# A graph layer with gathered node rows: paired gather buffers, node products in the first layer's tile, another order of the step, and lags taken in over the last 17 groups

## The chip, the cores and the metric

The kernel runs on one core of one Trainium2 chip. The metric is the device time of one execution in microseconds (us); the median over the runs counts. A second source is one execution taken by the hardware profiler, whose own time is given beside its span.

TensorE is called PE, VectorE DVE, ScalarE ACT, GpSimd POOL and SyncE SP, as in the profile. PEld is PE's loading of weights, which overlaps its products.

## The reference, cut to what matters

There are 12,500 nodes with 64 features (`x`) and 200,000 edges, sorted by their target node `dst`. Each edge has 64 features and a distance.

```python
nodes    = node_state[edges].reshape(num_edges, -1)      # x[src] beside x[dst]
gates    = ssp(edge_state @ We1 + be1) @ We2 + be2
gates    = gates * (1.0 - sigmoid(5.0 * (edges_distance - 3.5)))
h        = ssp(nodes @ Wn1 + bn1) @ Wn2 + bn2
sums     = zeros.at[edges[:, 1]].add(h * gates)
new      = node_state + (ssp(sums @ Ws1 + bs1) @ Ws2 + bs2)
out      = layernorm(x + new)
```

`ssp` is softplus minus log 2. All is in fp32.

## The kernel before

**Tiling.** The edges form 391 groups of 512, each with two halves of 256 and four slots of 128. As the edges are sorted by `dst`, the targets of a half lie in a window of 42 nodes that starts at a base held in `base_i`. The half of the first node layer that belongs to `dst` is computed once per node into a table in DRAM (`x @ Wn1[64:]`, L471), and 42 rows of it per half are loaded as weights (`wns`, L204). The row of `x` for `src` is gathered by GpSimd with an indirect DMA per slot (`gather`, L166 to L178), four per group. In one group of 32 the fourth slot is fetched row by row on SP instead (`fetch`, L180). A one-hot of each edge's place in its window stands in columns 64 to 105 of the same buffer (`onehot`, L209), so that one product with `wns` adds both halves of the node layer.

**One group's path.** `load` (SP: edge features and `wns`), `gather` (POOL), `onehot` (DVE), `transposes` (PE, L217, into a tx tile of PSUM), `xcopy` (ACT, L222), `layer1_edge` and `layer1_node` (PE, L226, L228, L233, into a z tile of two PSUM banks), `exps` and `logs` (ACT, L243, L246), `softplus` (DVE, L251), `layer2_edge` and `layer2_node` (PE, L257, L260, L265, into a gh tile), `hcut` and `message` (DVE, L270, L274), `scatter` (PE, L278: message times one-hot), `window` (DVE, L287: added to `sums` at the half's base). z, gh and tx have two buffers each; `xg`, which holds the gathered rows and the one-hot, has 25.

**Order.** The order of every engine is written out by hand (`manual_schedule`). One loop step i has groups at different stages: the scatter of group i-3, the second layer of i-1, the first layer of i+1, the transposes of i+3, and the gather of i+19. On PE the order in a step is L278, L257, L260, L226, L228, L233, L217, L265. The scatter writes into an unused part of the second bank of the z tile of i+1. From step `both` = 378 on, 12 groups before the last, the lags are cut at once: step 378 has no transposes and two second layers, step 379 three scatters, each into a tx tile of its own.

**Nodes.** When all edges of a block of nodes are done (`block_steps` gives the step, with a margin that the kernel checks), its `node_block` runs in five parts, one per loop step: `hidden` (PE, L306) with `clamp` (DVE, L314, L315, and SP's load of x, L312); `logs` (ACT, L318, L319) with `ssp` (DVE, L322); `layer2` (PE, L327, L330) with `center` (DVE, L334, L336, L337); the square (ACT, L341) and its sum (DVE, L345, L346); `root` (ACT, L350, L351) and `store` (DVE, L356 to L359, SP L360). Their products go into tx tiles. There is one block of 212 nodes, 23 of 512, and two of 256 at the end, whose parts take turns after the last step.

**Start.** Up to some 72 us the table is built, the windows' bases are found and the first 20 groups' gathers begin; the later 14 of these wait for a DVE memset in the table's loop (L171). A branch at the end of the program handles edges outside of their window; it is not taken with these data.

Of the kernel before, what the change touches and what calls it, by code (L numbers as in the profile page):

```python
# [31 lines left out]

# [19 lines left out]

P = 128
# [11 lines left out]
CATCH_UP = 12  # L65
# [7 lines left out]
def node_blocks(N):  # L73

    rest = N - NB
    first = rest % NB
    assert rest > 0 and first % 2 == 0 and first <= HE
    sizes = ([first] if first else []) + [NB] * (rest // NB) + [HE, HE]
    return [(sum(sizes[:i]), n) for i, n in enumerate(sizes)]
# [18 lines left out]
def gnn_resnorm_kernel(ctx: ExitStack, tc: tile.TileContext, a: dict, out: bass.AP, E: int):  # L98
# [52 lines left out]
    half = const.tile([P, 1], F32, name="half")  # L151
    ones3 = const.tile([PIECES, HE], BF16, name="ones3")
# [13 lines left out]
    def gather(g, after=False):  # L166

        xg = loads.tile([P, K, P], F32, name="xg", bufs=AHEAD + 5)
        xgs[g] = xg
# [61 lines left out]
    def layer1_node(g, h):  # L231
        zn = zs[g][:, h, HE * (1 - h) : HE * (2 - h)]
        nc.tensor.matmul(zn, wns[:, g % REST, h, :], xTs[g][:, h], start=True, stop=True, skip_group_check=True)  # L233
# [29 lines left out]
    def layer2_node(g, h):  # L263
        for t in range(2):
            nc.tensor.matmul(ghs[g][:, 1, 2 * t + h, :], ss[g][:, 1 + h, t, :], wn2, start=False,  # L265
                             stop=h == 1 and t == 1, skip_group_check=True)
# [5 lines left out]
    def message(g):  # L272
        msgs[g] = work.tile([P, K, D], F32, name="msg", bufs=3)
        nc.vector.tensor_mul(msgs[g], ghs[g][:, 0], hs[g])  # L274
# [6 lines left out]

    def window(g):
        for h in range(2):
            base = nc.values_load(base_i[0:1, 2 * g + h : 2 * g + h + 1], engines=[DVE], min_val=0, max_val=N - 1,
                                  skip_runtime_bounds_check_because="it was clamped to these bounds")
            part = sums[h * D : (h + 1) * D, bass.ds(base, W)]
            nc.vector.tensor_add(part, part, scs[g][h * D : (h + 1) * D, h * W : (h + 1) * W])  # L287

    def node_block(first, n, pool):
# [7 lines left out]
        def tile3(name):  # L297
            return pool.tile([P, 2, 2, D], F32, name=name, bufs=2)[:p, :nq]
# [11 lines left out]
        def clamp():  # L310
            t["y"] = tile3("y")
            nc.sync.dma_start(t["y"], x[rows, :].rearrange("(q p k) d -> p q k d", q=nq, k=2))  # L312
            t["l"], t["zb"] = (pool.tile([P, HE], F32, name=name, bufs=2) for name in ("l_s", "zb"))
# [19 lines left out]
        def center():  # L333
            nc.vector.scalar_tensor_tensor(t["y"], t["y"], 2.0, t["u"][:, :nq], OP.mult, OP.add)  # L334
            mean = small("mean")
            nc.vector.tensor_reduce(mean, t["y"], AX.X, OP.add)  # L336
            nc.vector.scalar_tensor_tensor(t["y"], mean.to_broadcast([p, nq, 2, D]), -1.0 / D, t["y"], OP.mult, OP.add)  # L337
# [5 lines left out]
        def variance():  # L343
            t["v"] = small("var")
            nc.vector.tensor_reduce(t["v"], t["y2"], AX.X, OP.add)  # L345
            nc.vector.tensor_scalar(t["v"], t["v"], 1.0 / D, EPS, OP.mult, OP.add)  # L346

        def root():
            t["r"] = small("rstd")
            nc.scalar.activation(t["r"], t["v"], AF.Ln)  # L350
            nc.scalar.activation(t["r"], t["r"], AF.Exp, scale=-0.5)  # L351

        def store():

            v, r = t["v"], t["r"]
# [3 lines left out]
            nc.vector.tensor_mul(t["y"], t["y"], r.to_broadcast([p, nq, 2, D]))  # L359
            nc.sync.dma_start(out[rows, :].rearrange("(q p k) d -> p q k d", q=nq, k=2), t["y"])  # L360

        def then(f, g):
            def both():
                f()
                g()
            return both

        return [(hidden, clamp), (None, then(logs, ssp)), (layer2, center), (None, then(square, variance)),
                (None, then(root, store))]

    def node_part(part):
        if part[0]:
            part[0](tx_tile())
        part[1]()

    with tc.manual_schedule():
# [4 lines left out]
        with tc.tile_pool(name="prep", bufs=1) as prep:  # L381
# [23 lines left out]
            nc.vector.memset(half, 0.5)  # L405
            nc.vector.memset(ones3, 1.0)
# [334 lines left out]
```

## Time and profile before

| what | value |
|---|---|
| runs, median of 3 | 2591.24 us |
| lowest and highest of the runs | 2576.13 and 2596.45 us |
| the profiled execution's own time | 1999.2 us |
| its span, first to last instruction | 1997.4 us |
| mean granted clock of PE in it | 0.986 |
| ACT busy | 919.0 us, 46% of the span |
| L251, softplus on DVE | 373.2 us, 392 instructions of 952 ns |
| L243, Exp on ACT | 317.4 us, 392 of 810 ns; idle before it 975.8 us, ended by PE |
| L217, transposes on PE | 283.5 us, 1552 of 283 ns; idle before it 69.9 us, most of it ended by gathers |

The profile's page gives, for each engine, its busy time, its share of the span and its instructions; then the span in 40 slices, with each slice's busy share in tenths; then groups of instructions, one per line of the kernel and shape, with busy time, mean duration and the idle time just before them with what ended it. In a group's name "out<-in" stands for the tiles written and read. Durations of PE's products overlap: the distance between starts is what a product costs, not its row's duration. A timeline shows start, duration, engine, line and tiles in order of time, and in brackets how long the engine had been idle and what released it. A table by windows gives each engine's busy time in a stretch, and the clock that PE was granted there.

### The profile page before, as it was taken

To read this page: it belongs to the slowest core of one execution; us is meant where nothing else is said; L and a number is where in the kernel's file an instruction comes from. 1 tells how busy PE (TensorE), PEld (TensorE's weight loads), DVE (VectorE), ACT (ScalarE), POOL (GpSimd) and SP (SyncE) were. 2 spreads that over 40 slices of the span, in tenths; PEclk is the share of its full clock that TensorE was granted. 3 is DMA by queue.
4 is the path that set the end of the run, shared out by engine and by line. 5 is a ranking of instruction groups with operands and counts; after the bars stand their busy time and mean duration, and the time that the engine had idled before them with its cause. 6 is when DMAs were issued, how large, how long until landed. Compare 5 with 4: busy or idle time off the path is not lost.

```text
span 1997.4 us, 42101 instructions
## 1 busy us (share of the span) xinstructions
PE 1881.8 (94%) x11378; PEld 1505.4 (75%) x11378; DVE 1050.5 (53%) x2752; ACT 919.0 (46%) x1322; POOL 1474.1 (74%) x1555
## 2 busy tenths in 40 slices
PE   4999999999999999999999999999999999999996
PEld 4888888887777777777777777777777877777775
DVE  4455555555544545545555555555554555555555
ACT  1344545454444444444444444444454554444433
POOL 7777777777777777777777777777777777777770
PEclk9999999999999999999999999999998999999988
DMA  8432222222223223232222322232222232223220
GB/s 231 140 68 68 66 69 68 67 67 69 66 68 69 58 66 69 62 70 61 63 68 64 69 65 64 68 69 69 68 65 68 64 71 68 68 71 68 68 61 25
DMA packets 171021, 143.15 MB, mean 72 GB/s; under 512 B 46507, under 2 KB 142947, under 8 KB 170778
## 3 DMA queue, kind: packets, MB, share of 16 engines
q1 hardware_dynamic: 119778, 87.95, 15.2%
q0 software_dynamic: 49632, 50.92, 14.2%
q8 instruction: 95, 1.56, 0.3%
q10 hardware_dynamic: 1368, 1.51, 0.3%
q14 instruction: 148, 1.21, 0.2%
HBM read 130.57 MB, written 9.63 MB: 70 GB/s over the span
## 4 chain that ended last, share of the span: by engine, by line
PE 58%; DMA 20%; POOL 7%; issue 6%; ACT 4%; DVE 3%; DVEq 1%; POOLq 0%; SPq 0%; ACTq 0%
DMA xg<-in_x,src_i 19%; PE gh L265 11%; PE z L233 9%; PE gh L260 8%; PE z L228 8%; POOL xg L176 7%; PE tx L217 6%; PE z L278 6%; PE gh L257 4%; PE z L226 3%; ACT u L246 2%; ACT u L243 2%; PE z L471 2%; DVE s L251 1%; DVE sums L287 1%
## 5 line engine op out<-in xcount | busy, mean ns | idle before, releaser
L176 POOL DMA_INDIRECT xg<-in_x,src_i x1551 | 1473.9, 950 | 476.8 <-issue 310.0
L251 DVE SCALAR_TENSOR_TENSOR s<-u,z 128x768 f32<-128x768 f32 x392 | 373.2, 952 | 842.6 <-ACT u L246 776.7
L243 ACT ACTIVATE u<-z 128x768 f32<-128x768 f32 x392 | 317.4, 810 | 975.8 <-PE z L233 975.8
L233 PE MATMUL z<-xT,wns 106*128 106x256 f32 x1564 | 410.0, 384 | 0.0
L265 PE MATMUL gh<-consts,s 128*128 128x64 f32 x3128 | 394.1, 269 | 0.0
L265 PEld LDWEIGHTS gh<-consts,s 128*128 128x128 f32 x3128 | 391.6, 196 | 0.1
L246 ACT ACTIVATE u<-u,one 128x768 f32<-128x768 f32 x392 | 366.1, 934 | 12.3
L217 PE MATMUL tx<-consts,xg 128*106 128x128 f32 x1552 | 283.5, 283 | 69.9 <-DMA xg<-in_x,src_i 63.9
L233 PEld LDWEIGHTS z<-xT,wns 106*128 106x128 f32 x1564 | 301.3, 193 | 44.4 <-issue 0.4
L217 PEld LDWEIGHTS tx<-consts,xg 128*106 128x106 f32 x1552 | 194.9, 133 | 164.9 <-DMA xg<-in_x,src_i 116.1
L260 PE MATMUL gh<-consts,s 128*128 128x128 f32 x1564 | 279.9, 301 | 0.0
L228 PE MATMUL z<-eT,consts 128*128 128x256 f32 x782 | 277.9, 437 | 0.0
L260 PEld LDWEIGHTS gh<-consts,s 128*128 128x128 f32 x1564 | 205.1, 191 | 89.0 <-issue 88.3
L278 PE MATMUL z<-xg,msg 128*128 128x84 f32 x1500 | 235.4, 279 | 0.0
L222 ACT COPY xT<-tx 106x512 f32<-106x512 f32 x391 | 221.6, 567 | 9.5 <-PE tx L217 9.1
L278 PEld LDWEIGHTS z<-xg,msg 128*128 128x128 f32 x1500 | 198.1, 192 | 0.0
L270 DVE TENSOR_TENSOR h<-gh,cut 128x256 f32<-128x256 f32 x391 | 166.0, 425 | 14.7 <-PE gh L265 2.2
L274 DVE TENSOR_TENSOR msg<-gh,h 128x256 f32<-128x256 f32 x391 | 166.0, 425 | 13.5
L228 PEld LDWEIGHTS z<-eT,consts 128*128 128x128 f32 x782 | 118.0, 190 | 47.6 <-issue 1.5
L287 DVE TENSOR_TENSOR sums<-sums,z 64x42 f32 x750 | 144.3, 192 | 13.0 <-issue 6.1
L257 PE MATMUL gh<-row,ones 3*128 3x512 bf16 x391 | 150.8, 386 | 0.0
L209 DVE TENSOR_TENSOR xg<-consts,rel 128x168 f32<-128x168 f32 x391 | 126.8, 325 | 1.1 <-issue 0.4
(79 smaller groups left out, 590.9 us busy)
## 6 DMA issues: line engine op xcount, KB each, us to landing
eT<-in_eT SPq DMA_DIRECT2D x391, 128.0 KB
xg<-in_x,src_i POOLq DMA_INDIRECT x1551
xr<-in_x SPq DMA_DIRECT2D x1536, 0.2 KB
wns<-table SPq DMA_DIRECT2D x782, 21.0 KB
table<-tb SPq DMA_DIRECT2D x14, 448.0 KB
sums<-in_xT SPq DMA_DIRECT2D x7, 455.0 KB
y<-in_x SPq DMA_DIRECT2D x23, 128.0 KB
out<-y SPq DMA_DIRECT2D x23, 128.0 KB
```

The source lines that it names most:

```text
L176: nc.gpsimd.indirect_dma_start(out=xg[:, k, :D], out_offset=None, in_=x, in_offset=bass.IndirectOffsetOnAxis(ap=src_i[:, g, k : k + 1], ax ...
L217: nc.tensor.transpose(tx[:, k, :], row, ident)
L222: nc.scalar.copy(xT, xTs[g])
L228: nc.tensor.matmul(zs[g][:, 0, :HE], we1.rearrange("a h d -> a (h d)"), eTs[g], start=False, stop=True, skip_group_check=True)
L233: nc.tensor.matmul(zn, wns[:, g % REST, h, :], xTs[g][:, h], start=True, stop=True, skip_group_check=True)
L243: nc.scalar.activation(us[g][:, part], z_of(g)[:, part], AF.Exp)
L246: nc.scalar.activation(us[g][:, part], us[g][:, part], AF.Ln, bias=one)
L251: nc.vector.scalar_tensor_tensor(ss[g].rearrange("p i t e -> p (i t e)")[:, part], us[g][:, part], BIG, z_of(g)[:, part], OP.min, OP.max)
L257: nc.tensor.matmul(gh, ones3[:, :P], row3.rearrange("q i k d -> q (i k d)"), start=True, stop=False, skip_group_check=True)
L260: nc.tensor.matmul(v[:, 0, t], ss[g][:, 0, t, :], we2, start=False, stop=False, skip_group_check=True)
L265: nc.tensor.matmul(ghs[g][:, 1, 2 * t + h, :], ss[g][:, 1 + h, t, :], wn2, start=False, stop=h == 1 and t == 1, skip_group_check=True)
L278: nc.tensor.matmul(sc, msgs[g][:, 2 * t : 2 * t + 2, :].rearrange("p h f -> p (h f)"), xgs[g][:, 2 * t : 2 * t + 2, D:DW], start=t == 0, s ...
```

## The change

- `gather` takes one buffer for two groups, 12 such buffers in all; at each even step it issues both groups' gathers (i+18 and i+19).
- On PE a step before the last 17 groups has the order L257, L260 (second edge layer), L226, L228 (first edge layer), node products, L233, L278 (scatter), L217, L265. Line numbers are those of before.
- A node block's products go into the free part of the z tile's second bank in place of a tx tile. A step with a node product has no scatter; the next one has two.
- A node block has eleven parts; x is loaded when the block is 5 groups from complete, and the others follow at the steps of `BLOCK_STEPS`.
- `ws2` and its bias have their mean taken off once at the start, and x is centred by itself; after the second product only an addition is left ahead of the square. The constant under the root is added by ACT.
- The lags are taken in bit by bit over the last 17 groups: two steps without transposes, one with two second layers, two with two scatters.
- The last block has 512 nodes. After the loop's last step an order by hand finishes the last group, with the window bases loaded beforehand.
- Two window bases are loaded by one instruction.

```diff
-CATCH_UP = 12
+CATCH_UP = 17
+PREPARE = 5
+BLOCK_STEPS = ((2, 3, 4, 4, 6, 7, 8, 9, 10, 14), (2, 3, 3, 4, 5, 6, 7, 8, 9, 10), (1, 1, 1, 2, 3, 3, 4, 4, 4, 4))
...
-        xg = loads.tile([P, K, P], F32, name="xg", bufs=AHEAD + 5)
-        xgs[g] = xg
+        if g % 2 == 0:
+            pair = loads.tile([P, 2, K, P], F32, name="xg", bufs=AHEAD // 2 + 2)
+            xgs[g], xgs[g + 1] = pair[:, 0], pair[:, 1]
+        xg = xgs[g]
...
+            mean = prep.tile([P, 3], F32, name="mean_w")
+            nc.vector.tensor_reduce(mean[:, :2], ws2, AX.X, OP.add)
+            nc.vector.tensor_reduce(mean[:1, 2:], brow[:, 3, :], AX.X, OP.add)
+            nc.vector.scalar_tensor_tensor(ws2, mean[:, :2].to_broadcast([P, 2, D]), -1.0 / D, ws2, OP.mult, OP.add)
+            nc.vector.scalar_tensor_tensor(brow[:, 3, :], mean[:1, 2:].to_broadcast([1, D]), -1.0 / D, brow[:, 3, :],
+                                           OP.mult, OP.add)
...
+                if i < ends:
                     for g in second[i]:
                         layer2_edge(g)
+                    if i >= -1:
+                        zs[i + 1] = z_tile()
+                        layer1_edge(i + 1)
+                        for f in tensor:
+                            f(zs[i + 1][:, 1, HE:])
+                        layer1_node(i + 1)
+                    done = [] if tensor else wait
+                    for n, g in enumerate(done):
+                        scatter(g, zs[i + 1][:, 1, HE + 2 * W * n : HE + 2 * W * (n + 1)])
                     at(exps, i + 1)
+                    at(logs, i + 1)
+                    for g in ahead[i]:
+                        transposes(g)
+                        xcopy(g)
+                    for g in second[i]:
+                        layer2_node(g)
                     at(softplus, i + 1)
+                    for g in done:
+                        window(g)
                     for g in second[i]:
                         hcut(g)
                         message(g)
+                else:
+                    for g in ahead[i]:
+                        transposes(g)
+                        xcopy(g)
+                    zs[i + 1] = z_tile()
+                    layer1_edge(i + 1)
+                    for f in tensor:
+                        f(zs[i + 1][:, 1, HE:])
+                    layer1_node(i + 1)
+                    exps(i + 1)
+                    logs(i + 1)
+                    for g in second[i]:
+                        layer2_edge(g)
+                        layer2_node(g)
+                        hcut(g)
+                        message(g)
+                    softplus(i + 1)
+                    done = wait
+                    for g in done:
+                        scatter(g, tx_tile()[:, : 2 * W])
+                        window(g)
...
+            begun.pop(2).others()
+            transposes(last)
+            xcopy(last)
+            zs[last] = z_tile()
+            layer1_edge(last)
+            layer1_node(last)
+            for some in (edge, node):
+                exps(last, some)
+                logs(last, some)
+            for g in range(last - 2, last + 1):
+                window_bases(g)
+            layer2_edge(last - 1)
+            layer2_node(last - 1)
+            scatter(last - 2, tx_tile()[:, : 2 * W])
+            softplus(last, edge)
+            hcut(last - 1)
+            message(last - 1)
+            layer2_edge(last)
+            scatter(last - 1, tx_tile()[:, : 2 * W])
+            softplus(last, node)
+            window(last - 2)
+            layer2_node(last)
+            window(last - 1)
+            hcut(last)
+            message(last)
+            scatter(last, tx_tile()[:, : 2 * W])
+            window(last)
+            for part in begun:
+                node_part(part)
```

## The prediction

> **What bounds the kernel now.** I read the busy shares and slices first, then the groups, then the waits of TensorE (PE) by stage, then single steps in the timeline. The page:
>
> ```profile
> PE 1881.8 (94%) x11378; PEld 1505.4 (75%) x11378; DVE 1050.5 (53%) x2752; ACT 919.0 (46%) x1322; POOL 1474.1 (74%) x1555
> ...
> PEclk9999999999999999999999999999998999999988
> ...
> L176 POOL DMA_INDIRECT xg<-in_x,src_i x1551 | 1473.9, 950 | 476.8 <-issue 310.0
> ```
>
> PE looks like the bound at 94%, but GpSimd's (POOL's) gathers sit beside it: 950 ns busy and about 0.30 us idle each. The timeline of POOL shows that the 0.30 us is part of the price:
>
> ```profile
> 306.71 0.94 POOL L176 DMA_INDIRECT xg<-in_x,src_i  x1 [0.30 <-issue]
> 307.95 0.95 POOL L176 DMA_INDIRECT xg<-in_x,src_i  x1 [0.30 <-issue]
> 309.20 1.02 POOL L176 DMA_INDIRECT xg<-in_x,src_i  x1 [0.30 <-issue]
> ```
>
> One gather every 1.25 us, four per group of 512 edges: 5.0 us per group. The first gathers, which wait for no buffer, have the same spacing. 1551 x 1.25 = 1939 us; they start at 3.3 us and the last begins at 1950.2 us, so POOL waits for some 8 us in all. A PE step, from one L226 to the next:
>
> ```profile
> 330.23 0.28 PE L226 MATMUL z<-ones,be 3*128 3x256 bf16 x1
> ...
> 334.63 0.28 PE L226 MATMUL z<-ones,be 3*128 3x256 bf16 x1
> ```
>
> 4.40 us. So PE is the bound only until it has used up the groups gathered ahead of it. The waits of PE from 71 to 480 us have 0.3 us on gathers; from 480 to 1900 us they read:
>
> ```profile
> PE tx L217 <- DMA xg<-in_x,src_i: 62.8, 152, 1.3
> PE tx L330 <- DVE l_s L322: 0.5, 2, 0.3
> ```
>
> From 480 us the gathers set the pace. Node products wait for nothing to speak of. The end is a third stage. By windows (columns: PE, PEld, DVE, ACT, POOL busy, granted clock, DMA share, GB/s):
>
> ```profile
> 1890.00:1919.00 29.00, 26.87 (x170) 21.30 (x167) 15.59 (x43) 13.48 (x20) 21.80 (x24) 1.00 0.28 65
> 1919.00:1934.00 15.00, 14.15 (x48) 10.61 (x48) 5.68 (x16) 3.85 (x6) 11.34 (x13) 0.55 0.32 76
> 1934.00:1981.00 47.00, 42.25 (x265) 33.19 (x265) 29.02 (x78) 21.08 (x35) 13.17 (x14) 1.00 0.13 29
> 1981.00:1997.40 16.40, 4.99 (x18) 3.25 (x18) 6.92 (x26) 3.17 (x10) 0.00 (x0) 0.53 0.07 18
> ```
>
> For 15 us the clock is halved; PE falls behind the gathers and never catches up. The last group's transposes start at 1968.8 us, 16 us after its gather landed (1950.2 plus some 2.6).
>
> **The median is another matter.** The profiled execution took 1999.2 us, 1.8 more than its span; the runs' median is 2591.24, 592 us more. No row explains that. Two readings fit: a slower PE (72 us start + 391 x 4.41 + 25 node blocks x 1.9 + 28 us end = 1871; 2591 asks for a mean clock near 0.72), or a slower gather ((2591 - 50)/1551 = 1.64 us). I work each edit in us of the profile, then ask what it is under either reading.
>
> **The change, part by part.**
>
> *Pairs of groups in one xg buffer.* Still 1551 gathers of the same shape at 1.25 us: 0. Per pair one wait for a free buffer in place of two; as the spacing is 1.25 us with or without a wait, that gives 0. Room falls from 25 groups to 24. Gathers i+18 and i+19 now wait for the scatter of group i-5, done in step i-2, or i-1 where it is put off; their transposes come in step i+15 or later, at least 15 x 4.4 = 66 us on, against 8 x 1.25 = 10 us of gathering. Cost 0. If even groups now wait for both groups' gathers, PE runs 5 us later without a change of pace; the last group (390) has no partner.
>
> *Order of PE's step.* Second-layer edge product first, first layer next, scatter after it. Same matmuls. Starts taken from the trace in the PE-bound stretch: before, L265 to L278 0.11, L278 to L257 0.21, L233 to L217 0.215: 0.535 us. After, L265 to L257 should be 0.21 (L260 to L226, also a switch from fp32 to bf16, is 0.21), L233 to L278 0.215 (the wide matmul lasts that long), L278 to L217 0.11: 0.535. Ends: -0.02 (L278's second matmul starts 17 ns late today) to +0.1 us per step (one weight load of 0.107 us uncovered). I take 0.
>
> [...] The scatter (four matmuls, 0.56 us) now follows the first layer into the second bank of the tile that Exp (L243) reads. So Exp must wait for the scatter: 0.56 us after the first layer. By the trace that costs nothing: today the same 0.56 us precede the first layer, and ACT idles 975.8/391 = 2.5 us before each Exp. The cover is the step between softplus and its reader: softplus ends near 998.9 us, its second layer starts at 1002.1. Only a delay over 3 us would reach PE. [...] by the trace 0, which I take.
>
> *Node products in the z tile.* No tx buffer for 50 products: today's waits for it are under 1 us. The scatter is put off one step, the next does two: 0.56 us moved, not added. Node parts spread over 10 to 14 steps instead of 5, hidden under PE or gathers; uncovered, a block's chain is about 12 us, and only the last is. SP's y loads come 5 groups earlier and the store 4 steps after its data; SP no longer waits in front of eT and wns loads. 0.
>
> *DVE.* Two window bases per load, half the loads; DVE is 53% busy: 0, but about 0.36 us in the last window.
>
> *Start.* Four small DVE instructions to centre ws2 and its bias, about 1 us by L336 and L337 (0.42 and 0.43 at twice the width). POOL waits 1.33 us there for L171's memset, behind DVE. 0 to +1; I take +0.5.
>
> *Lags over 17 groups.* Today one step does two second layers, the next three scatters through two tx buffers:
>
> ```profile
> 1918.28 0.65 PE L278 MATMUL tx<-xg,msg 128*128 128x84 f32 x4 [0.92 <-DVE sums L287]
> 1919.85 0.65 PE L278 MATMUL tx<-xg,msg 128*128 128x84 f32 x4 [0.92 <-DVE sums L287]
> 1920.42 0.39 PE L226 MATMUL z<-ones,be 3*128 3x256 bf16 x1
> ```
>
> 1.84 us of waits, then matmuls at half clock (L226 0.39 against 0.28): 15 us at 0.55 lose 15 x 0.45 = 6.8 us. [...] The trace shows waits of 0.92 us and a stretch of thin work before the drop. [...] I take that it goes, and keep 6.8 us for the range. Walking the PE products of the last 30 groups (transposes 0.44, first layer 1.61, second 1.80, scatter 0.56, node products 0.86 and 0.96; group g landing at 1953 - 5 x (390 - g)), today's order ends transposes(390) at 1959.9 without clock drop (measured 1969.3 with it), the new at 1957.0. So -12.3: 6.8 clock, 3 from the walk, the rest other small waits that I take to go too.
>
> *After the last transposes.* Today 1997.4 - 1969.3 = 28.1 us. New, by durations of today's rows with hand-offs: copy 0.7, first layer 0.9, Exp and Ln 1.5, softplus 0.7, second layer 0.95, h and message 1.0, scatter 0.7, window 0.5, hidden 1.0, clamp to ssp 2.2, layer 2 0.75, add, square, reduce 1.45, root and scale 1.6, store to end 5.0 = 19, plus 1.5 if the clock is halved again: 20.5. Gain 7.6: one block of 512 instead of two of 256 in turn, the mean and its subtraction (L336 and L337, 0.29 each) taken out, x loaded early.
>
> Sum in the profiled execution: +0.5 - 12.3 - 7.6 = -19.4, giving **1978 us**. In the runs: if PE is slow, the walk's gain is 2 us, as PE is behind anyway, plus 8; if the gather is slow, PE is not behind, 2 plus 8. So about -10, with 0 to 7 for the clock: -11. **2591 - 11 = 2580 us.**
>
> **Rivals.**
>
> 1. *Only the end moves, little* (forecast): 2580, own range 2565 to 2594. Chance 0.62.
> 2. *The end is dearer than the profile shows* (faster by over 1%). If the runs have a low clock through the last 75 us, today's three scatters and two end blocks cost about twice their 19 us: 2591 - 38 = 2553. For: the clock is 0.53 to 0.55 in two of the end's windows. Against: most of the end's chain is DVE, ACT and DMA, which no clock row touches. Chance 0.14.
> 3. *A weight load comes uncovered on PE* (slower). Place: L265 to L257, or L278 to L217. Price up to 0.107 us per step; it decides where the runs are PE-bound and the price passes 26/391 = 0.07 us, or 37/391 = 0.095 against the end's gain. Full price: 391 x 0.107 = 42 us, at a clock of 0.72 58 us: 2638. For: today's L228 pair shows such a load uncovered (0.32 us between starts, where L233 has 0.215). Against: of the three new neighbours two are fp32 after fp32, and the third has the 0.21 us of its kind. Chance 0.12.
> 4. *The change doesn't do what it says*: another wait halves the clock at the end, nothing gained: 2591. Chance 0.12.
>
> **How the numbers follow.** About 1% is what a measurement of this kernel can tell from no change: the three runs spread over 0.8%. Over 1% faster: case 2's 0.14 and a little of 1: 0.15. Over 1% slower: case 3's 0.12 and what I have overlooked among the new waits: 0.17. Within: 0.68. The range 2555 to 2612 takes in case 4, most of 2, and case 3 to half its price.
>
> **What would show it.** Right: gathers still 1.25 us apart, the last beginning near 1950 us; PE steps of 4.40 us before 480 us; no waits of L278 on DVE at the end; about 20 us from the last transposes to the end; span near 1978. Wrong: PE steps over 4.47; gathers held by buffers; Exp so late that DVE's softplus holds L260; a clock row at 0.5 that lasts.

## The result, and the profile after

| | before | after |
|---|---|---|
| runs, median | 2587.75 us (4 runs, 2576.13 to 2596.45) | 2794.32 us (4 runs, 2781.81 to 2800.46) |
| ratio, with its 95% interval | | 1.0795 (1.0736 to 1.0855) |
| profiled execution's own time, span | 1999.2, 1997.4 us | 2791.51, 2789.7 us |
| mean granted clock of PE in it | 0.986 | 0.808 |

Slower by 8%; forecast was -0.4%, with 2612 us as the upper end.

Whole sets of executions, before and after alike, came in one of two conditions, one in which all engines issue normally (before takes some 2000 us) and one, called **slow issue** here, in which TensorE and SyncE issue slowly for stretches (before takes some 2590 us), and the runs of the result are of the second while the profile that the prediction read is of the first. Each ratio below is taken within one set.

The page of after, the lines that answer to those shown of before:

```profile
PE 2265.7 (81%) x11373; PEld 1804.8 (65%) x11373; DVE 1051.5 (38%) x2745; ACT 926.8 (33%) x1317; POOL 1477.8 (53%) x1555
...
PEclk9888788878777978888778868788878787778896
...
L185 POOL DMA_INDIRECT xg<-in_x,src_i x1551 | 1477.6, 953 | 1169.0 <-PE tx L226 434.3
```

Every engine is idler than in the profile of before, and the clock never stays at 9. A gather still takes 0.95 us, but POOL is idle for 1169 us where it was idle for 477; of that, 396 us are the 0.30 us between two gathers, and where a releaser is named it is mostly PE. So the gathers no longer set the pace: they wait for buffers that PE hands back late. The names of releasers are less certain here than in the profile of before, as they are inferred from semaphore updates, and this trace holds 19,078 of these against 54,283.

What PE does in that time, by its timeline (start, duration, then the idle time before it and its cause):

```profile
126.88 1.38 PE L277 MATMUL gh<-consts,s 128*128 128x64 f32 x6
129.10 0.27 PE L277 MATMUL gh<-consts,s 128*128 128x64 f32 x1 [0.85 <-issue]
131.90 0.27 PE L277 MATMUL gh<-consts,s 128*128 128x64 f32 x1 [2.54 <-issue]
134.72 0.58 PE L268 MATMUL gh<-row,ones 3*128 3x512 bf16 x1 [2.55 <-issue]
```

The products come 2.8 us apart, and the profile shows no wait between them. In the same stretches SP's register instructions last 0.70 us; their median is 0.037 us. 243 of 2318 such instructions (FUSED_REGOPS) last over 0.6 us in after, none in the profile of before. The expectations below speak of all engines; the trace shows slow issue of PE and SP alone. Inside such stretches ACT's Ln follows its Exp after 0.03 us as always (57 pairs), and POOL's gathers keep their 1.25 us.

After the last gather (2646.1 us) nothing issues slowly any more. By windows (PE, PEld, DVE, ACT, POOL busy, clock, DMA share, GB/s), from the last gather to the end:

```profile
2646.00:2676.00 30.00, 27.79 (x125) 21.67 (x126) 15.19 (x44) 11.48 (x18) 0.95 (x1) 0.73 0.16 44
2676.00:2731.00 55.00, 52.87 (x333) 40.02 (x332) 30.17 (x81) 26.86 (x40) 0.00 (x0) 1.00 0.18 51
2731.00:2790.00 59.00, 41.92 (x148) 30.32 (x146) 21.54 (x65) 13.06 (x25) 0.00 (x0) 0.55 0.03 8
```

Without gathers PE is 96% busy at full clock. The last 59 us at about half clock are a second matter, the end.

### The profile page after: what moved, and what is told of

Same layout as the page of the kernel before. It is cut to its first block, busy times and chain, and to the rows that moved or that the text cites. A ratio compares the mean times of both kernels' runs of the same rounds, so it can differ in the third digit from the quotient of the medians.

```text
span 2789.7 us, 41243 instructions
## 1 busy us (share of the span) xinstructions
PE 2265.7 (81%) x11373; PEld 1804.8 (65%) x11373; DVE 1051.5 (38%) x2745; ACT 926.8 (33%) x1317; POOL 1477.8 (53%) x1555
## 5 line engine op out<-in xcount | busy, mean ns | idle before, releaser
L277 PE MATMUL gh<-consts,s 128*128 128x64 f32 x3128 | 465.3, 292 | 113.0 <-issue 112.3
L277 PEld LDWEIGHTS gh<-consts,s 128*128 128x128 f32 x3128 | 452.9, 218 | 135.4 <-issue 134.9
L243 PE MATMUL z<-xT,wns 106*128 106x256 f32 x1564 | 519.6, 463 | 22.3 <-DMA wns<-table 10.6
L243 PEld LDWEIGHTS z<-xT,wns 106*128 106x128 f32 x1564 | 362.9, 237 | 106.3 <-issue 18.3
L257 ACT ACTIVATE u<-u,one 128x768 f32<-128x768 f32 x392 | 365.8, 933 | 12.7
L237 PE MATMUL z<-eT,consts 128*128 128x256 f32 x782 | 334.5, 516 | 12.7 <-DMA eT<-in_eT 8.4
L271 PE MATMUL gh<-consts,s 128*128 128x128 f32 x1564 | 331.3, 343 | 9.0 <-DVE s L262 9.0
L226 PE MATMUL tx<-consts,xg 128*106 128x128 f32 x1552 | 289.3, 310 | 52.0 <-issue 45.1
L271 PEld LDWEIGHTS gh<-consts,s 128*128 128x128 f32 x1564 | 245.6, 224 | 118.3 <-issue 106.2
L290 PEld LDWEIGHTS z<-xg,msg 128*128 128x128 f32 x1480 | 261.8, 226 | 44.8 <-issue 16.6
L226 PEld LDWEIGHTS tx<-consts,xg 128*106 128x106 f32 x1552 | 220.3, 163 | 66.8 <-issue 51.4
L268 PE MATMUL gh<-row,ones 3*128 3x512 bf16 x391 | 170.2, 435 | 101.0 <-DVE h L282 31.6
L237 PEld LDWEIGHTS z<-eT,consts 128*128 128x128 f32 x782 | 139.6, 224 | 72.5 <-issue 29.0
L306 DVE TENSOR_TENSOR sums<-sums,z 64x42 f32 x740 | 142.9, 193 | 24.6 <-issue 9.5
```

The source lines that it names most:

```text
L226: nc.tensor.transpose(tx[:, k, :], row, ident)
L237: nc.tensor.matmul(zs[g][:, 0, :HE], we1.rearrange("a h d -> a (h d)"), eTs[g], start=False, stop=True, skip_group_check=True)
L257: nc.scalar.activation(us[g][:, part], us[g][:, part], AF.Ln, bias=one)
L268: nc.tensor.matmul(gh, ones3[:, :P], row3.rearrange("q i k d -> q (i k d)"), start=True, stop=False, skip_group_check=True)
L271: nc.tensor.matmul(v[:, 0, t], ss[g][:, 0, t, :], we2, start=False, stop=False, skip_group_check=True)
L290: nc.tensor.matmul(sc, msgs[g][:, 2 * t : 2 * t + 2, :].rearrange("p h f -> p (h f)"), xgs[g][:, 2 * t : 2 * t + 2, D:DW], start=t == 0, s ...
```

## The experiments

### Without slow issue: parts one by one

The first four expectations were written for runs of about 2590 us; this set took about 2000 us.

The kernel before, unchanged.

> The kernel before, unchanged, for its trace at the runs' own time. Theory 1 (stretches in which the engines issue one instruction per 0.7 us, as in the trace after, are common to both kernels, and the profile of 1999 us was one without them): a time near 2590 us, a mean clock near 0.8 to 0.9, SP instructions of 0.7 us in clusters of several hundred us in total. Rival (the slow stretches come with the change): no such instructions, clock 0.98, and the 592 us lie somewhere else.

Measured: 2002.02 us, ratio 0.9998 (0.9968 to 1.0028). None of SP's register instructions lasts over 0.6 us; clock 0.980.

The changed kernel with a buffer for each group:

```diff
-            pair = loads.tile([P, 2, K, P], F32, name="xg", bufs=AHEAD // 2 + 2)
+        xg = loads.tile([P, K, P], F32, name="xg", bufs=AHEAD + 5)
...
-                if i > 0 and i % 2 == 0:
-                    at(gather, i + AHEAD - 2)
+                if i > 0:
                     at(gather, i + AHEAD - 1)
```

> The changed kernel with one xg buffer per group (25 of them) and a gather per step, as before. If the pairs of groups cost the time: near 2590. If the order of the step and the tail cost it: near 2794. Half each: 2690.

Measured: 2011.89 us, ratio 1.0071 (1.0045 to 1.0097).

The kernel before with the pairs alone (the same lines the other way round):

> The kernel before with the pairs of groups in one xg buffer alone. If the pairs cost the time: near 2790. If not: near 2590.

Measured: 2002.63 us, ratio 1.0014 (0.9981 to 1.0046).

The kernel before with the order of PE's step alone (the scatter's loop moved from ahead of L257 to behind L233):

> The kernel before with PE's new order alone: second edge layer, first layer, then the scatter, node products still in a tx tile. If the order costs the time, by a late Exp or an uncovered weight load: 2650 to 2790. If not: near 2590, and a PE step of 4.40 us wherever PE is neither held nor at a lower clock.

Measured: 1994.89 us, ratio 0.9975 (0.9948 to 1.0002).

What follows: with normal issue the pairs and the order cost nothing, as forecast, but the gain of 20 us at the end did not come: 12 us were lost instead. The timeline of the single-buffer variant, where its end goes wrong:

```profile
1949.10 0.70 PE L235 MATMUL z<-eT,consts 128*128 128x256 f32 x2
...
1950.77 0.48 DVE L338 TENSOR_SCALAR l_s<-z,consts 128x256 f32<-128x256 f32 x1
...
1951.29 0.42 ACT L342 ACTIVATE l_s<-l_s 128x256 f32<-128x256 f32 x1 [2.79 <-DVE l_s L338]
...
1952.15 0.56 ACT L229 COPY xT<-tx 106x512 f32<-106x512 f32 x1
...
1952.77 2.08 PE L241 MATMUL z<-xT,wns 106*128 106x256 f32 x4 [2.97 <-ACT xT L229]
```

Clamp and `logs` of a late node block stand in one step. DVE comes to the clamp last, ACT waits 2.79 us for it, the copy of the transposes stands behind it on ACT, and with the short lag of the last steps PE waits 2.97 us for that copy. From 1951.4 us on, in the midst of that wait, the clock is halved for 59.1 us, to the end:

```profile
1919.00:1934.00 15.00, 13.69 (x90) 10.33 (x88) 9.18 (x28) 7.22 (x10) 11.33 (x13) 1.00 0.31 81
1934.00:1951.00 17.00, 15.39 (x92) 11.16 (x91) 9.72 (x27) 7.69 (x12) 10.57 (x12) 1.00 0.12 24
1951.00:1978.00 27.00, 24.13 (x81) 17.52 (x82) 8.23 (x24) 8.11 (x12) 0.00 (x0) 0.51 0.02 5
1978.00:2008.40 30.40, 17.90 (x61) 12.96 (x60) 10.89 (x35) 4.91 (x12) 0.00 (x0) 0.50 0.04 12
```

The old drop at 1919 us is gone (clock 1.00), and a longer one stands 32 us later.

### Under slow issue: the change again, the end mended, the node products alone

The changed kernel, unchanged.

> The changed kernel unchanged. Its trace in the result has stretches, some 990 us together, in which all engines issue slowly (0.70 us for a register instruction of SP); none of the four runs of the call before had one. Theory 1 (the 206 us of the result come with these stretches and not with the order of the work): where the kernel before takes about 2000 us, this one takes 2010 to 2016, ratio 1.005 to 1.008, as the single-buffer variant did. Theory 2 (the pairs of groups, which the variant left out, cost it): over 2100 us, with gathers that wait for buffers.

Measured: 2797.38 us against 2583.63 us, ratio 1.0818 (1.0713 to 1.0923). The set came with slow issue, so the expectation for 2000 us was not put to the test. The changed kernel was never timed with normal issue; the single-buffer variant stands in for it.

The changed kernel with ACT's copies first in the last 17 steps:

```diff
+                if i >= ends:
+                    turn(i + 1)        # transposes and xcopy of the next step
                 for g in ahead[i]:
                     at(onehot, g + 2)
                 for part in now:
                     part.others()
```

> The changed kernel with one thing moved in its last 17 steps: on ACT, the copy of the next step's transposes goes ahead of the node parts of this step. Nothing else moves on PE. Theory A (in step 385 the copy stands behind the node block's Exp, which waits for DVE's clamp; PE waits 2.97 us, its clock halves and stays so for the last 59 us): the wait goes, the clock stays at 1.00 up to the last transposes, the last transposes come at 1962 to 1966 instead of 1978.2, the span ends near 1987; 1985 to 1995 us in the runs, 15 to 25 us below the changed kernel. Rival B (the thin work of the end halves the clock anyway, at the next small wait): within 5 us of the changed kernel, with the half clock beginning a few us later.

Measured: 2808.25 us, ratio 1.0799 (1.0673 to 1.0926). The whole says nothing. But what follows the last gather is free of slow issue and can be compared. First the changed kernel, then the one with copies first, the last stretch of each:

```profile
2724.00:2780.00 56.00, 42.03 (x140) 30.47 (x140) 17.79 (x55) 11.97 (x22) 0.00 (x0) 0.50 0.03 9
```

```profile
2757.00:2805.00 48.00, 33.63 (x125) 25.25 (x124) 17.85 (x55) 11.45 (x21) 0.00 (x0) 0.56 0.04 10
```

From the last gather to the end it is 142.1 us against 133.4: 8.7 us less, with 17 groups to go in both. The half clock of the end begins later and lasts 44.2 us in place of 59.3. So the copy's place is part of it. It holds in the other traces: with copies first the clock of the end is halved for 44.3 us in one and for 33.2 us, in two pieces, in another; without, for 54.8 to 59.3 us in five. Just ahead of where it is halved then, PE has a second wait for the same late block, at its second product:

```profile
2761.67 0.74 PE L356 MATMUL z<-consts,l_s 128*128 128x128 f32 x4 [2.56 <-DVE l_s L348]
```

This wait stands in all three traces with copies first, and the clock is halved about 1 us after it ends. That this wait halves it was not tested. Both theories were half right.

The kernel before with the node products of the main part in the z tile, the scatter put off by a step:

```diff
+                early = bool(part and part[0] and 0 <= i < both)
+                wait += third[i]
+                done = [] if early else wait
...
+                    if early:
+                        part[0](zs[i + 1][:, 1, HE:])
```

> The kernel before with one part of the change: the node products of the main part go into the free half of the z tile's second bank, the scatter of that step is put off to the next. Theory (this part costs nothing): ratio 0.997 to 1.003 to the kernel before. Rival (a step with two scatters makes PE late and stops the gathers): ratio above 1.005, and waits of the gathers for buffers of 10 us or more. If the slow stretches come again, this run's profile shows how the kernel before, whose main loop it shares, spends its time in them: theory 1 expects the same 0.70 us instructions in it, and a PE step shorter than the 6.3 us of the changed kernel.

Measured: 2718.88 us, ratio 1.0434 (1.0296 to 1.0573). Not free. The edit does three things: another tile, a later scatter, and node products that stand ahead of L233 in the step instead of behind it.

### Under slow issue: before's own profile, the order, the node products back in tx

The kernel before, unchanged.

> The kernel before, unchanged, for its profile. Where it takes about 2585 us: theory 1 ([...]engines issue one instruction in 0.70 us for stretches) expects such stretches in it too, a mean clock near 0.82 and PE idle for some 300 us (2585 us less 1871 us of PE work at a clock of 0.815, 2296 us), against 500 in the changed kernel. Where it takes about 2000 us: no instruction of SP's registers over 0.6 us, clock 0.98.

Measured: 2598.01 us, ratio 0.9998 (0.9971 to 1.0025); 180 of the 2318 SP instructions last over 0.6 us. The page of its profiled execution, which took 2621.65 us:

```profile
PE 2217.7 (85%) x11378; PEld 1755.6 (67%) x11378; DVE 1046.8 (40%) x2752; ACT 919.5 (35%) x1322; POOL 1471.9 (56%) x1555
...
PEclk9879878778778879887888868887788778888888
...
L176 POOL DMA_INDIRECT xg<-in_x,src_i x1551 | 1471.7, 949 | 1015.3 <-issue 375.2
```

So before suffers from the same thing. PE is idle for 2619.9 - 2217.7 = 402 us here and for 2789.7 - 2265.7 = 524 us in after. The two profiled spans differ by 170 us: 122 are more idle time of PE, 48 more busy time (clock 0.825 and 0.808). The medians differ by 207 us; this execution of before took 24 us over its median.

The order of PE's step alone, as above:

> The kernel before with the new order of PE's step alone (edge product of the second layer, first layer, then the scatter). Where the kernel before takes about 2585 us: theory O (Exp now also waits for the scatter, the first second-layer product comes 0.56 us earlier in the step, so softplus has over 1 us less to spare before its reader; that is free where nothing is late, and costs where ACT and DVE stop for 5 to 20 us): 2650 to 2700 us, with PE waiting for DVE's s ahead of L260. Rival Z (only the node products in the z tile, with 2719 us by themselves, and the spread of the node parts cost time): within 1% of before. Where before takes about 2000 us: ratio 0.995 to 1.000, as measured once.

Measured: 2575.19 us, ratio 0.9877 (0.9845 to 0.9909). Theory O was wrong, and the order gains about 1%: 1.2% by this ratio, 0.9% by the medians of all executions. Of the versions run in both conditions it is the one that was no slower than before in either.

The changed kernel with the node products in tx tiles, and beside it the one with copies first again:

```diff
-                        for f in tensor:
-                            f(zs[i + 1][:, 1, HE:])
                         layer1_node(i + 1)
+                        for f in tensor:
+                            f(tx_tile())
...
-                    done = [] if tensor else wait
+                    done = wait
```

> The changed kernel with the node products of the main part in tx tiles again, no scatter put off; everything else as changed. Where the kernel before takes about 2585 us: rival Z expects 2650 to 2670 (2797 less the 135 us that the part cost by itself); theory O expects that most stays, 2740 or more. Where before takes about 2000 us: 2005 to 2015, as the end is untouched.

> The changed kernel with ACT's copies ahead of its node parts in the last 17 steps, once more. Where before takes about 2585 us it was 2808 against 2797 and says nothing, as slow issue hides the end: 2780 to 2815 again. Where before takes about 2000 us: theory A (the copy behind the node block's Exp holds PE for 2.97 us, after which its clock is halved for the last 59 us) expects the clock at 1.00 to the last transposes, these at 1962 to 1966, the end near 1987 in the profile, 1985 to 1995 us in the runs; rival B (thin work halves it anyway) 2007 to 2017.

Measured: 2857.84 us, ratio 1.1022 (1.0947 to 1.1096), and in the same set the changed kernel with copies first at 2876.31 us, 1.110 (1.1021 to 1.1178). The number is what theory O expected, but O itself had fallen with the run of the order. So taking out a part that cost 135 us on the kernel before gives back 18 us here, against a neighbour whose end is the shorter one. The neighbour itself had come at 1.080 in the set before: ratios of different sets can differ by three points for one kernel.

### Under slow issue: the pairs

The pairs alone on the kernel before; the changed kernel with a buffer for each group and copies first; and the changed kernel with a buffer for each group, but two groups' gathers issued at even steps:

```diff
+        xg = loads.tile([P, K, P], F32, name="xg", bufs=AHEAD + 5)
...
                 if i > 0 and i % 2 == 0:
                     at(gather, i + AHEAD - 2)
                     at(gather, i + AHEAD - 1)
```

> The kernel before with one buffer for two groups of gathered rows and both groups' gathers issued at even steps; nothing else. Where the kernel before takes about 2590 us: theory P (neither the order of PE's step, 0.988 by itself, nor the tile of the node products, 1.10 without it, makes the change slow; the pairs are left) 2750 to 2850 us, ratio 1.06 to 1.10, with more stretches of slow issue than before has. Rival S (the node parts, spread over more steps and with their loads elsewhere, or the windows' bases cost it): within 1.5% of before. Where before takes about 2000 us: ratio 0.998 to 1.005, as measured once.

Measured: 2877.82 us, ratio 1.1077 (1.1018 to 1.1137). One edit, with a ratio of 1.0014 with normal issue, costs 10.8% here, just over theory P's range and no less than the whole change.

> The changed kernel with a buffer for each group and its gather at each step, as before, and with ACT's copies ahead of its node parts in the last 17 steps. Where before takes about 2590 us: theory P 2540 to 2610 us, ratio 0.98 to 1.01, as what is left of the change costs nothing; rival S over 2750. Where before takes about 2000 us: theory A (the copy behind the node block's Exp halves the clock for the last 59 us) 1985 to 1995 us, against 2012 without the move; rival B (thin work halves it anyway) 2007 to 2017.

> The changed kernel with a buffer for each group, 25 of them, as before, but both groups' gathers still issued at even steps. It tells apart what in the pairs costs time. If it is that eight gathers come in a row[...]: as the changed kernel, ratio 1.07 to 1.11 where before takes about 2590 us. If it is the shared buffer (one wait for two groups' release, room for 24): ratio 0.98 to 1.02. Where before takes about 2000 us: as the variant with a gather at each step, 2007 to 2017.

Measured: 2708.29 us, 1.0426 (1.037 to 1.0481), and 2716.00 us, 1.0483 (1.0404 to 1.0562). Without pairs the change still costs over 4%, between the two expectations. The order in which POOL's program has the gathers does not matter: it is the buffer's release that starts them.

The timelines of POOL under slow issue, the kernel before first, then the pairs:

```profile
1513.75 0.94 POOL L176 DMA_INDIRECT xg<-in_x,src_i  x1 [2.41 <-PE z L228]
...
1517.50 0.94 POOL L176 DMA_INDIRECT xg<-in_x,src_i  x1 [0.30 <-issue]
1519.91 0.95 POOL L176 DMA_INDIRECT xg<-in_x,src_i  x1 [1.47 <-DVE xg L209]
```

```profile
1503.45 0.94 POOL L178 DMA_INDIRECT xg<-in_x,src_i  x1 [15.46 <-PE z L280]
...
1512.20 0.94 POOL L178 DMA_INDIRECT xg<-in_x,src_i  x1 [0.30 <-issue]
1518.70 0.94 POOL L178 DMA_INDIRECT xg<-in_x,src_i  x1 [5.56 <-PE z L280]
```

One release lets four gathers run, or eight. I counted unbroken runs (a gap of over 1.6 us between starts ends one) in each trace from 200 us on:

| under slow issue | ratio | runs of four | runs of eight |
|---|---|---|---|
| before, new order of PE's step | 0.988 | 325 | 10 |
| before | 1 | 239 | 51 |
| after, single buffers, copies first | 1.043 | 222 | 60 |
| before, node products in z | 1.043 | 136 | 101 |
| after, single buffers, two groups' gathers issued together | 1.048 | 228 | 56 |
| after | 1.080 | 0 | 164 |
| after, copies first | 1.080 and 1.110 | 0 | 161 and 163 |
| after, node products in tx | 1.102 | 0 | 167 |
| before, pairs | 1.108 | 0 | 167 |

The put-off scatters bring 50 more runs of eight to the kernel before (51 to 101), and the changed kernel with single buffers has 50 more than the new order alone (60 and 10): two scatters in one step hand back two groups at once. There are 50 node products. With pairs nearly all runs are of eight already and the put-off adds none, which may be why taking it out gained so little there.

Where in a run the slow instructions lie: the share of SP's register instructions (FUSED_REGOPS and MOVE) that last over 0.5 us, by the time since the run's first gather:

```
us since the run began    0-2   2-4   4-6   6-8   8-10  10-12  12-14
before, runs of four      0.02  0.08  0.14  0.00
before, runs of eight     0.01  0.09  0.27  0.36  0.37  0.14
pairs, runs of eight      0.01  0.10  0.25  0.49  0.45  0.11   0.00
after, runs of eight      0.02  0.12  0.24  0.33  0.25  0.08   0.00
```

It rises until near the last gather and is back at nothing about 2 us after it. PE's products per us in the pairs' trace fall from 5.1 (6 to 8 us) to 2.8 (10 to 12).

### Breaking the run by hand

The pairs with a pause of POOL between the two groups; four groups in one buffer; the new order of PE's step with pauses after each second gather.

```diff
+    def pause(n):
+        for _ in range(n):
+            nc.gpsimd.memset(idle, 0.0)
...
                     at(gather, i + AHEAD - 2)
+                    pause(4)
                     at(gather, i + AHEAD - 1)
```

```diff
+        if g % 4 == 0:
+            four = loads.tile([P, 4, K, P], F32, name="xg", bufs=AHEAD // 4 + 1)
```

```diff
+            if k % 2 == 1:
+                pause(pauses)
...
-                    at(gather, i + AHEAD - 1)
+                    at(gather, i + AHEAD - 1, False, 2)
```

> The kernel before with pairs (2878 against 2597 us where the issue is slow), and between the two groups of a pair POOL fills a scratch tile four times with zeros, so that it gathers four times, pauses, and gathers four times. The shared buffer and its one release for two groups stay. In the traces SP's slow instructions come late in an unbroken run of gathers (share 0.01 in its first 2 us, 0.45 after 6 us in runs of eight) and end with it. Theory R (length of the run is what costs, 2.4 us for each two runs of four that join into eight): where before takes about 2590 us, 2590 to 2700, ratio 1.00 to 1.04, with the slow share in a run's last part at 0.15 as in runs of four. Rival W (the shared buffer costs by what waits for it): 2850 to 2900, ratio 1.10. Where before takes about 2000 us the gathers set the pace, and the pauses come on top: 2150 to 2350.

> The kernel before with four groups in one buffer, 24 groups in all, and their sixteen gathers issued every fourth step. Theory R: runs of sixteen, some 90 of them; where before takes about 2590 us at least as slow as the pairs and by the price of a joined run (2.4 us times 84) near 3080: 2900 to 3150, ratio 1.12 to 1.21. Rival W': what counts is that gathers are released by PE at all, not how many at once: 2860 to 2900, as the pairs. Where before takes about 2000 us: 1995 to 2015, no difference.

> The kernel before with the new order of PE's step (0.988 by itself) and with two short fills of a scratch tile by POOL after each second gather: runs of two instead of four. Theory R: less slow issue than in runs of four, so PE's step comes down from 6.3 us; where before takes about 2590 us 2400 to 2540, ratio 0.93 to 0.98, a slow share under 0.05. Rival N (all gathers cost alike, however they are spaced, or runs of four are short enough): 2560 to 2600. Where before takes about 2000 us: the pauses come on top of the gathers, 2200 to 2500.

> The kernel before with pairs and POOL's pause of some 1.4 us between the two groups of a pair, once more. Where before takes about 2590 us (pairs without the pause 2878, ratio 1.108): theory R (the unbroken run of eight gathers costs) 2590 to 2700, ratio 1.00 to 1.04; rival W (the shared buffer's one release costs, whatever the run) 2850 to 2900, ratio 1.10. Where before takes about 2000 us: 2232 again, which tells nothing of this question.

Measured, all with normal issue: 2232.41 us, ratio 1.1183 (1.1136 to 1.123); 2001.83 us, 1.0015 (0.9991 to 1.0039); 2501.23 us, 1.2537 (1.2486 to 1.2588), just over what was expected; the last, the first once more, 2239.05 us, 1.1162 (1.11 to 1.1225). The gathers set the pace, the pauses (1.44 us for four fills) come on top of them, and sixteen gathers per buffer cost nothing. One of the twenty executions with sixteen took 3045.99 us at a mean clock of 0.54; it is not in the ratio, there is no trace of it, and its cause is not known. As said beforehand, these runs tell nothing of slow issue. **Whether a pause in the run gives the time back there was not seen.**

## Why the prediction was wrong

**The step that failed** is "pairs of groups in one xg buffer ... Cost 0". It was worked out from a profile in which POOL is never stopped: "Still 1551 gathers of the same shape at 1.25 us", and a lead of 66 us against 10 us of gathering. With normal issue that holds (1.0014, and four groups per buffer 1.0015). The runs to be forecast had slow issue. There PE is behind by the whole lead (the transposes of 17 groups are left when the last gather begins), POOL waits for buffers, and the size of a release decides how the gathers come: 1.108 by itself on the kernel before, and in the changed kernel with copies first 1.080 and 1.110 with pairs against 1.043 without (three sets). I had the warning: 592 us that no row of the profile explained. I then priced each edit "in us of the profile" and asked only what a slower PE or a slower gather would make of it, not which wait would end last if PE were the slow one. Two signs of being wrong that the prediction had named appeared, gathers held by buffers and a clock row at 0.5 that lasts; the first belongs to slow issue and not to the change, as POOL is idle for 1015 us in before under slow issue, too.

**The 592 us**, read as a clock near 0.72 or a gather of 1.64 us. Neither: a gather in a run is still 1.25 us, the clock is 0.825, and PE is idle for 402 us. Of the 622 us between the two profiled spans of before, 336 are more busy time of PE and 287 more idle time. The lower clock was part of it, slow issue was not thought of.

**"Node products in the z tile: 0.56 us moved, not added".** With slow issue 1.043 by itself. What moved is also a release: two groups' buffers come free at once. But the waits of PE (us in total, times, longest) show the larger part, PE standing at a block's second node product, in that run and then in before under slow issue:

```profile
PE z L330 <- DVE l_s L322: 87.3, 16, 7.0
PE tx L330 <- DVE l_s L322: 7.7, 9, 1.8
```

In the profile that I read that wait was 3.7 us. The wait at the first node product (L306 on `sums`) grew as well, from 3.9 to 29.6 us. Together that is 105 us more, of the 135 us that the edit costs. In the whole change, where the node parts are spread over more steps, the wait at the second product is 0.4 us, so this price does not carry over to it.

**"Order of PE's step: 0"** was right with normal issue (0.9975), and so was the reading of Exp: it now waits for the scatter (in the single-buffer variant 326 of its waits, 785.1 us in all, end with the scatter), comes 0.41 us later in the step and costs nothing. Rival 3 (a weight load uncovered, up to +42 us) is out: PE's step between 75 and 450 us has a median of 4.350 us, against 4.407 before. So the term is not 0 but a gain of 0.057 us per step: from the start of a scatter to the next product it is 0.41 us instead of 0.56, from the second node layer to the next product 0.93 instead of 0.84. With normal issue the gathers hide it. Under slow issue, with PE the late one, 391 steps of it would be 22 us (an estimate from these steps), and the medians differ by 24 us; that this is the cause was not tested. The order also leaves 10 runs of eight where there were 51; why, I did not follow up.

**"Lags over 17 groups: -12.3".** The two waits at L278 went, and so did the drop at 1919 us, as the prediction had taken from its row; no run changed these waits alone. But at PE's new wait of 2.97 us the clock is halved once more, for 59 us: at the end the prediction's rival 4 came true. In the 3.41 us ahead of the drop (the shortest stretch of one clock in before and after) PE was idle for 1.6 us, and for 1.8 us (the two waits of 0.92 us) ahead of the old one. I read the old drop from its row and failed to ask the same of the new schedule: which waits of PE does it bring? Two parts of one block in one step, on two engines, with the copy behind them.

**"After the last transposes: 28.1 to 20.5".** In the single-buffer variant it is 2008.5 - 1979.3 = 29.2 us. The sum took full clock or 1.5 us for half; at half clock PE's parts there take nearly twice as long (first layer's node product 2.07 us where it is 1.03 at full clock), and two groups' second layers stand in turn, not one.

So with normal issue, too, the change loses: +0.7% in the variant without pairs, against -1.0% in the profile's sum. With slow issue the parts do not add up: 1.108, 1.043 and 0.988 give 1.14 multiplied, and the whole is 1.08.

**Shown and argued.** Shown: the pairs alone make 10.8%, and nothing with normal issue; slow instructions lie in the late part of runs of gathers and stop after them; the put-off adds 50 runs of eight.

Argued: that the long run is how the pairs cost their time. For it: each added run of eight is worth (2877.8 - 2597.2) / (167 - 51) = 2.4 us with the pairs and (2718.9 - 2583.6) / 50 = 2.7 us with the node products. In before under slow issue, PE's second step after the start of a run takes 9.4 us on average for runs of eight and 5.7 us for runs of four.

Against it: in the same trace the time from one run's start to the next is 6.28 us per group for runs of eight and 6.52 for runs of four, so over the whole run nothing seems lost. Most of the 2.7 us is the wait at the node products. The new order takes 41 runs of eight away and gains 24 us, 0.6 us for each; the changed kernel with single buffers has nine more than before and costs 111 us. So the number of long runs does not put the table in order.

Open: how the pairs cost their time; what the 4% without pairs is (PE waits 145 us there for DVE's `h` and `sums` ahead of the second layer, which was not tested); what slow issue is; and why one set of executions has it and another, on the same chip, does not.

## What to carry to other kernels

When the runs take much longer than the profiled execution, first find which engine would have to be late for that, and price each edit in that regime too: an edit that is free while gathers never wait can be the dearest one once they wait for buffers. A shared buffer is a shared release: ask how much work starts at once when it comes free. And in a short-lag tail, keep the copy that PE waits for ahead of everything on its engine that waits for another engine.

## What the runs showed of the hardware

**Slow issue.** In stretches of up to 32 us in the trace of after (slow SP instructions less than 5 us apart) PE and SP issue slowly, SP one register instruction in 0.70 us, PE one product with its weights in 2.8 us. The stretches come with the gathers: in after the last slow register instruction starts at 2639.2 us, the last gather at 2646.1 us. ACT, DVE and POOL do not show it: there ACT's Ln follows its Exp after 0.03 us, DVE's register instructions last 0.10 us at most, as in the profile of before, and POOL's gathers keep their 1.25 us. With normal issue 1515 gathers run without a break in the profile of before, and none of this is seen: SP's register instructions (FUSED_REGOPS) last 0.051 us at most. The trace of after holds 19,078 semaphore updates, the profile of before 54,283; whether that has to do with slow issue was not shown. Two chips ran a set with slow issue and a set without, so it is not the chip alone.

**The clock.** The granted clock is 1.0 or 0.5 in the profiles of before and after, and all its stretches except the one cut off by the end are multiples of 3.41 us (14 stretches in before, 204 in after). Ahead of the last drop in the traces of before, of the single-buffer variant and of the first run with copies first, PE was idle for 2.5, 1.6 and 2.4 us of 3.41. ACT's Exp (0.81 us) and DVE's softplus (0.95 us) last as long in after at half clock as at full.

**PE's products** overlap: in the profile of before one of the second node layer (L265) lasts 0.275 us, with 0.112 us from start to start.

**POOL's fill** of a tile of 128 x 256 fp32 takes 0.32 us, four of them 1.44 us.
